# One row tile in ninety fetched row by row by SyncE instead of by a GpSimd gather

## The chip, the cores and the metric

The kernel runs on one core of a Trainium2 chip. The core has five engines that run side by side, each with its own instruction queue, executed in order: TensorE (PE, matrix products and transposes), VectorE (DVE), ScalarE (ACT), GpSimd (POOL) and SyncE (SP, which here only issues transfers). Sixteen DMA engines move the data between the large memory (HBM) and the on-chip memory (SBUF)[...]. Engines signal one another by semaphores. The metric is the device time of one execution in microseconds (us), the median of several runs.

## The reference

A recommender model scores 16,384 samples. Each sample has 69 fields, and each field names a row of an embedding table of 100,001 rows of 96 floats (384 bytes). A label names one more row, the query.

```python
u = emb[batch_user]                      # 16384 x 69 x 96
q = broadcast(emb[batch_label])
z = concatenate([q, u, q - u, q * u])
h = dice(z @ W1 + b1, a1)                # 384 -> 64
att = (h @ W2 + b2) @ W3 + b3            # one weight per row
pre = where(batch_user < ITEM_NUM, u * att, 0)
pooled = einsum('gf,bfe->bge', window, pre)       # 10 groups of fields
x = concatenate([pooled, ql])            # 11 * 96
# two more dense layers with dice (200, 80), then one output
```

So more than 1.1 million rows of the table are read at random places, and everything else is done on them.

## The kernel before

**Tiling.** The samples are cut into 32 blocks of 512 (`NBLK`, `BLK`). A block has 69 chunks (`NCH`): a chunk is 512 embedding rows, four row tiles of 128 rows, one row per SBUF partition. In the 64 main chunks of a block a chunk holds 64 fields of 8 samples; the other five chunks of a block hold one of the last fields for all 512 samples. Altogether there are 2208 chunks or 8832 row tiles. A step of the plan handles two chunks, so there are 1104 steps (`NPAIR`), 34.5 to a block.

**One step.** `fetch` (L301) allocates a row buffer `u` of eight row tiles and, for each of them, issues a gather on GpSimd (L312, through the helper `gather` at L256 to L262, so that its instructions stand under L257) and a TensorE transpose (L313) of the 128 x 96 tile into PSUM. A gather is an indirect DMA: GpSimd reads 128 indices from a column of the index tile `ids`, and the rows land on 128 partitions. After four transposes VectorE multiplies the chunk by the query (`quT`, L316) and ScalarE copies it (`uT`, L325). Two steps later `hidden` (L328) makes the hidden layer from both, ScalarE and VectorE finish it (L344 to L346); three and more steps later the attention weights are made (`attend_rows`, `spread`), and seven steps later (`POOL_LAG`) `pool` (L387) multiplies the row tiles, read a second time from `u`, by the weights (L397). The pool of row buffers has 14 of them (`upool`, L130). When a block is complete its dense layers (`top1` and after, L427 on) are spread over the next ten steps.

**Order of work.** The order is written out by hand: `at(step, ...)` (L530) puts pieces of work into a plan, and the plan is emitted step by step (L594). Each engine gets its instructions in that order; what an engine does next depends on its own queue and on the semaphores alone. The kernel's transfers are issued by two engines: GpSimd issues all gathers (8832 of row tiles, and 128 of label rows in `head_gather`, L271, four per block, 14 steps ahead of the block), SyncE issues the index loads, the weights at the start and the two stores at the end. `load_ids` (L144) loads the indices of four blocks at once into one of two buffers, 20 steps ahead of the first of these blocks (L565).

Of the kernel before, what the change touches and what calls it, by code (L numbers as in the profile page):

```python
# [1 line left out]

# [7 lines left out]

F32 = mybir.dt.float32
I32 = mybir.dt.int32
AF = mybir.ActivationFunctionType
ALU = mybir.AluOpType
PSUM = bass.MemoryType.PSUM

P = 128
B, F, E, G = 16384, 69, 96, 10  # L40
ITEM_NUM = 100000
# [5 lines left out]
NBLK = B // BLK  # L47
FM = 64
NTAIL = F - FM
NS = BLK // FM  # L50
NMAIN = BLK // NS
NCH = NMAIN + NTAIL
# [12 lines left out]
EARLY = 20  # L65

CLOSE = 8


class Pack:  # L70


    def __init__(self, **shapes):
        self.places, self.width = {}, 0
        for name, (row, n, m) in shapes.items():
            self.places[name] = slice(row, row + n), slice(self.width, self.width + m)
            self.width += m
# [37 lines left out]
def rec_kernel(  # L115
# [3 lines left out]
    idx: bass.AP,  # L119
    emb: bass.AP,  # L120
    rows: bass.AP,
    near: bass.AP,
    far: bass.AP,
    out: bass.AP,
):
    nc = tc.nc

    const = ctx.enter_context(tc.tile_pool(name="const", bufs=1))
    ipool = ctx.enter_context(tc.tile_pool(name="ipool", bufs=2))
# [10 lines left out]

    ids = {0: const.tile([P, NCOL], I32, name="ids0")}
    nc.sync.dma_start(out=ids[0], in_=idx0)

    def load_ids(n):  # L144

        t = ipool.tile([P, NIDS, NCOL], I32, tag="ids", name=f"ids{n}")
        nc.sync.dma_start(out=t.rearrange("p b n -> p (b n)"), in_=idx[(n - 1) // NIDS])
        for k in range(NIDS):
            ids[n + k] = t[:, k, :]


    wn = const.tile([P, NEAR.width], F32, name="wn")
    nc.sync.dma_start(out=wn, in_=near)
# [3 lines left out]
    ident = const.tile([P, P], F32, name="ident")  # L157
# [26 lines left out]
    for i in range(2):  # L184
        t = const.tile([E + 1, BLK], F32, name=f"qT{i}")
# [70 lines left out]
    def gather(table, dst, index):  # L256
        nc.gpsimd.indirect_dma_start(  # L257
            out=dst,
            out_offset=None,
            in_=table,  # L260
            in_offset=bass.IndirectOffsetOnAxis(ap=index, axis=0),
        )  # L262

    def chunk(c):

        n, k = divmod(c, NCH)
        if n == NBLK - 1 and k >= EARLY:
            k = NMAIN + k - EARLY if k < EARLY + NTAIL else k - NTAIL
        return n, k

    def head_gather(n):  # L271

# [28 lines left out]
    def fetch(i, between=None):  # L301

        u = upool.tile([P, 8, E], F32, tag="u", name=f"u{i}")
        uT = []
        quT = tpool.tile([E, 2, 512], F32, tag="quT", name=f"quT{i}")
        for j in range(2):
            if j == 1 and between:
                between()
            n, k = chunk(2 * i + j)
            ptr = ps_tr.tile([E, 512], F32, tag="tr", name=f"ptr{i}_{j}")  # L310
            for t in range(4):
                gather(rows, u[:, 4 * j + t, :], ids[n][:, 4 * k + t : 4 * k + t + 1])  # L312
                nc.tensor.transpose(ptr[:, t * P : (t + 1) * P], u[:, 4 * j + t, :], ident)  # L313
            q = qTs[n % 2][0:E]
            if k < NMAIN:
                nc.vector.tensor_tensor(  # L316
                    quT[:, j, :].rearrange("e (s f) -> e s f", f=FM),
                    ptr.rearrange("e (s f) -> e s f", f=FM),
                    by_field(q[:, k * NS : (k + 1) * NS]),
                    ALU.mult,  # L320
                )
            else:
                nc.vector.tensor_tensor(quT[:, j, :], ptr, q[:, 0:BLK], ALU.mult)
            uT.append(room(k))
            nc.scalar.copy(uT[j][0:E], ptr)  # L325
        return u, uT, quT

    def hidden(i, uT, quT):  # L328

        ph = ps_h.tile([P, 512], F32, tag="h", name=f"ph{i}")  # L330
        places = [chunk(2 * i + j) for j in range(2)]
        sums = [ph[j * H1 : (j + 1) * H1, :] for j in range(2)]
        for (n, k), p in zip(places, sums):
            if k >= NMAIN:
                nc.tensor.matmul(p, Cq, qTs[n % 2], start=True, stop=False)  # L335
        for j, ((n, k), p) in enumerate(zip(places, sums)):
            if k < NMAIN:
                nc.tensor.matmul(p, As[n % 2][:, k // 4, :], uT[j], start=True, stop=False)  # L338
            else:
                nc.tensor.matmul(p, A, uT[j][0:E], start=False, stop=False)  # L340
        for j, p in enumerate(sums):
            nc.tensor.matmul(p, Wp, quT[:, j, :], start=False, stop=True)  # L342
        y = ypool.tile([P, 512], F32, tag="y", name=f"y{i}")
        nc.scalar.activation(y, ph, AF.Sigmoid, scale=S_DICE)  # L344
        nc.scalar.activation(y, y, AF.Identity, bias=a1c, scale=na1c)  # L345
        nc.vector.tensor_mul(y, ph, y)  # L346
        return y
# [9 lines left out]

    def attend_tail(i, j, y, uT):

        n, k = chunk(2 * i + j)  # L360
        pa = ps_x.tile([E, 512], F32, tag="x", name=f"pa{i}_{j}")
        nc.tensor.matmul(pa, vrep[j * H1 : (j + 1) * H1, :], y[j * H1 : (j + 1) * H1, :], start=True, stop=True)  # L362
        nc.vector.scalar_tensor_tensor(pres[n][:, k - NMAIN, :], pa, bb[0:E], uT[j][0:E], ALU.add, ALU.mult)  # L363
# [23 lines left out]
    def pool(i):  # L387

        u, rw = us.pop(i), rws.pop(i)
        todo = [(j, *chunk(2 * i + j)) for j in range(2)]  # L390
        todo = [(j, n, k) for j, n, k in todo if k < NMAIN]
        if not todo:
            return
        pa = ps_acc.tile([E, 2, NS, G], F32, tag="acc", name=f"acc{i}")
        for j, n, k in todo:
            for t in range(4):
                nc.tensor.matmul(  # L397
                    pa[:, j, 2 * t : 2 * t + 2, :].rearrange("e n g -> e (n g)"),
                    u[:, 4 * j + t, :],
                    rw[:, t, j, :],  # L400
                    start=True,
                    stop=True,
                )
        if len(todo) == 2:
            _, n, k = todo[0]
            nc.vector.tensor_copy(  # L406
                pooled[n][:, :, k * NS : (k + 2) * NS].rearrange("e g s -> e s g"),
                pa.rearrange("e j s g -> e (j s) g"),
            )
        else:  # L410
            j, n, k = todo[0]
            nc.vector.tensor_copy(
                pooled[n][:, :, k * NS : (k + 1) * NS].rearrange("e g s -> e s g"), pa[:, j]
            )

    def dice(x, g, p, b, weights):

        sb, sa, sna = weights
        nc.scalar.activation(g, p, AF.Sigmoid, bias=sb, scale=S_BN * S_DICE)
        nc.scalar.activation(g, g, AF.Identity, bias=sa, scale=sna)  # L420
        nc.vector.scalar_tensor_tensor(x, p, b, g, ALU.add, ALU.mult)  # L421
# [78 lines left out]
    def pool_of(k):  # L500
        return lambda: pool(k)
# [4 lines left out]
    def tails_of(k):  # L506
        def work():
            uT = hs.pop(k)[0]
            for j in range(2):
                if chunk(2 * k + j)[1] >= NMAIN:  # L510
                    attend_tail(k, j, ys[k], uT)

        return work

    def fetch_of(k, between=()):
        def work():
            for j in range(2):
                n = chunk(2 * k + j)[0]
                if n not in pooled:
                    pooled[n] = bpool.tile([E, G, BLK], F32, tag="pooled", name=f"pooled{n}")  # L520
                    pres[n] = xpool.tile([E, NTAIL, BLK], F32, tag="pre", name=f"pre{n}")
            u, uT, quT = fetch(k, lambda: [w() for w in between])
            us[k], hs[k] = u, (uT, quT)

        return work
# [3 lines left out]

    def at(step, *work):  # L530
        plan.setdefault(step, []).extend(work)

    c = NPAIR - CLOSE
    for i in range(c):
# [6 lines left out]
        if i >= 2:  # L541
            at(i, hidden_of(i - 2))
        if i < c - CLOSE:
            if i >= POOL_LAG:
# [16 lines left out]
    for n in range(NBLK):  # L561
        first, end = n * NCH // 2, ((n + 1) * NCH - 1) // 2
        if n > 0:
            if n % NIDS == 1:
                at(first - 20, lambda n=n: load_ids(n))  # L565
            at(first - 14, lambda n=n: qs.__setitem__(n, head_gather(n)))
            at(first - 11, lambda n=n: head_turn(n, qs.pop(n)))
            at(first - 9, lambda n=n: head_rows(n))
        if n < NBLK - 2:
            for s, work in enumerate(top_steps(n, slice(0, BLK))):  # L570
                at(end + POOL_LAG + 4 + s, work)
        elif n == NBLK - 2:
            for s, work in enumerate(top_steps(n, slice(0, BLK))):
                at(end + POOL_LAG + s // 2, work)
# [9 lines left out]
    d = NPAIR  # L584
# [75 lines left out]
```

## Time and profile before

| what | value |
|---|---|
| median of 3 runs | 11251.05 us (11247.6 to 11253.1) |
| span of the profiled execution, first to last instruction | 11239.3 us |
| lies around the span (median less span) | 11.75 us |
| TensorE busy, share of the span | 9082.8 us, 81% |
| GpSimd busy | 8465.4 us, 75% |
| VectorE, ScalarE busy | 3014.3 us, 3188.3 us |
| row gathers on GpSimd | 8832, 945 ns each |
| from issue of a gather to its landing, median | 2.5 us |
| share of the 16 DMA engines taken by the gathers | 18.7% |
| granted clock of TensorE, mean | 0.727 |

The time of the profiled execution is known as its span; no other time of that execution is given, and the runs of the median are executions of their own.

A row of a group of instructions reads: line, engine, operation, what it writes and reads, how many; busy time in us and mean duration in ns; then the engine's idle time just ahead of them, and what ended most of that idle time. "issue" there means that nothing the profile shows was waited for. A row of the list of waits reads: who waited, for whom, total us, how often, the longest in us. A row of the timeline begins with start and duration in us, and the brackets hold the idle time ahead. "SPq" is SyncE's issuing of transfers, which isn't counted as busy.

### The profile page before, as it was taken

The numbers are of one execution on the slowest core, as the hardware profiler recorded it, in microseconds if no ns is written. First come the engines' busy times: TensorE is split into PE (matmuls) and PEld (weight loads), VectorE is DVE, ScalarE is ACT, GpSimd is POOL, SyncE is SP. The second block draws the span as 40 slices with busy tenths as digits, with TensorE's granted clock in tenths as the row PEclk, the third lists the DMA queues.
The fourth block names the chain that finished last, engine by engine and source line by source line (L and its number), as shares of the span: only waits on it lengthen the run. The fifth ranks groups of instructions, "written<-read, shape, count | busy, mean of one in ns | idle before, by whom it ended". The sixth has DMA issues, their size and how long they took to land.

```text
span 11239.3 us, 108444 instructions
## 1 busy us (share of the span) xinstructions
PE 9082.8 (81%) x41797; PEld 4395.1 (39%) x41797; DVE 3014.3 (27%) x5325; ACT 3188.3 (28%) x4969; POOL 8465.4 (75%) x8966
## 2 busy tenths in 40 slices
PE   7888888888878787877888778777787887888888
PEld 3333433333433333333333333333343333433335
DVE  3222222222222222222222222222222222222222
ACT  2222222222222222222222222222222222222223
POOL 7777777777777777777777777777777777777776
PEclk6767777677776777777777777777777767777767
DMA  2111111111111111111111111111111111111111
GB/s 49 40 40 40 40 40 42 40 40 40 40 42 40 40 40 40 42 40 40 40 40 42 40 40 40 40 42 40 40 40 40 42 40 40 40 40 40 40 40 35
DMA packets 288946, 454.19 MB, mean 40 GB/s; under 512 B 143538, under 2 KB 143922, under 8 KB 288306
## 3 DMA queue, kind: packets, MB, share of 16 engines
q0 software_dynamic: 286720, 440.98, 18.7%
q8 instruction: 335, 5.49, 0.2%
q1 hardware_dynamic: 1714, 6.28, 0.2%
q14 instruction: 177, 1.45, 0.0%
HBM read 446.61 MB, written 0.07 MB: 40 GB/s over the span
## 4 chain that ended last, share of the span: by engine, by line
POOL 51%; issue 23%; PE 15%; DMA 11%; ACT 0%; DVE 0%; POOLq 0%
POOL u L257 50%; DMA u<-in_rows,ids 11%; PE p L438 4%; PE acc L397 3%; PE ph L342 2%; PE ph L338 2%; PE ptr L313 2%; POOL q L257 1%; PE prow L353 1%; PE ph L335 1%; PE ph L340 0%; PE pc L290 0%; PE pa L362 0%; PE patt L370 0%; PE p L449 0%
## 5 line engine op out<-in xcount | busy, mean ns | idle before, releaser
L257 POOL DMA_INDIRECT u<-in_rows,ids x8832 | 8343.6, 945 | 2690.9 <-issue 2510.2
L313 PE MATMUL ptr<-ident,u 128*96 128x128 f32 x8832 | 2092.4, 336 | 2080.2 <-DMA u<-in_rows,ids 2066.4
L325 ACT COPY uT<-ptr 96x512 f32<-96x512 f32 x2208 | 1285.2, 582 | 4422.4 <-DVE quT L316 4069.1
L313 PEld LDWEIGHTS ptr<-ident,u 128*96 128x96 f32 x8832 | 1184.6, 150 | 2904.1 <-DMA u<-in_rows,ids 2460.6
L397 PEld LDWEIGHTS acc<-rw,u 128*96 128x96 f32 x16384 | 1746.1, 190 | 1206.4 <-issue 1059.7
L346 DVE TENSOR_TENSOR y<-ph,y 128x512 f32<-128x512 f32 x1104 | 763.5, 692 | 4885.1 <-ACT y L345 4703.4
L316 DVE TENSOR_TENSOR quT<-ptr,qT 96x512 f32<-96x512 f32 x2048 | 1375.9, 677 | 2183.2 <-PE ptr L313 2180.0
L397 PE MATMUL acc<-rw,u 128*96 128x20 f32 x16384 | 1852.9, 260 | 23.1 <-DVE rw L375 18.0
L338 PE MATMUL ph<-uT,A 128*64 128x512 f32 x4096 | 1688.2, 902 | 1.0 <-ACT uT L325 1.0
L342 PE MATMUL ph<-quT,wn 96*64 96x512 f32 x4416 | 1628.4, 809 | 0.0
L344 ACT ACTIVATE y<-ph 128x512 f32<-128x512 f32 x1104 | 659.4, 597 | 2971.7 <-PE ph L342 2962.3
L345 ACT ACTIVATE y<-y,wn,na1c 128x512 f32<-128x512 f32 x1104 | 898.1, 814 | 37.3
L342 PEld LDWEIGHTS ph<-quT,wn 96*64 96x64 f32 x4416 | 447.5, 191 | 1070.4 <-issue 1069.8
L438 PE MATMUL p<-pooled,wf 96*100 96x512 f32 (+1 forms) x1400 | 706.2, 654 | 0.0
L338 PEld LDWEIGHTS ph<-uT,A 128*64 128x64 f32 x4096 | 269.0, 179 | 616.0 <-issue 609.8
L406 DVE COPY pooled<-acc 96x160 f32<-96x160 f32 x1008 | 419.9, 417 | 129.4 <-PE acc L397 129.4
L353 PE MATMUL prow<-y,v 128*32 128x512 f32 x2208 | 452.4, 894 | 0.3 <-DVE y L346 0.3
L438 PE MATMUL p<-pre,V 96*100 96x512 f32 (+1 forms) x700 | 398.9, 717 | 2.7 <-DVE x L421 2.3
L438 PEld LDWEIGHTS p<-pooled,wf 96*100 96x100 f32 x1400 | 265.6, 202 | 341.2 <-issue 341.2
L375 DVE SCALAR_TENSOR_TENSOR rw<-patt,bb,wn 128x320 f32<-128x320 f32 x554 | 277.8, 543 | 221.2 <-PE patt L370 220.3
L355 ACT COPY row<-prow 128x512 f32<-128x512 f32 (+1 forms) x277 | 161.8, 584 | 314.5 <-PE prow L353 314.2
L370 PE MATMUL patt<-ident,row 128*128 128x128 f32 x1108 | 231.2, 347 | 15.9 <-DVE pre L363 15.2
(66 smaller groups left out, 2227.6 us busy)
## 6 DMA issues: line engine op xcount, KB each, us to landing
u<-in_rows,ids POOLq DMA_INDIRECT x8832, 2.5
ids<-in_idx SPq DMA_DIRECT2D x8, 560.0 KB, 3.7
q<-in_emb,ids POOLq DMA_INDIRECT x128, 2.5
wf<-in_far SPq DMA_DIRECT2D x1, 1209.0 KB, 7.8
wn<-in_near SPq DMA_DIRECT2D x1, 236.0 KB, 2.7
ids<-in_idx SPq DMA_DIRECT2D x1, 140.0 KB, 2.2
out<-r SPq DMA_DIRECT2D x1, 63.5 KB
out<-r SPq DMA_DIRECT2D x1, 0.5 KB
```

The lines of the kernel that those rows point to most:

```text
L257: nc.gpsimd.indirect_dma_start(out=dst, out_offset=None, in_=table, in_offset=bass.IndirectOffsetOnAxis(ap=index, axis=0),)
L313: nc.tensor.transpose(ptr[:, t * P : (t + 1) * P], u[:, 4 * j + t, :], ident)
L316: nc.vector.tensor_tensor(quT[:, j, :].rearrange("e (s f) -> e s f", f=FM), ptr.rearrange("e (s f) -> e s f", f=FM), by_field(q[:, k * NS ...
L325: nc.scalar.copy(uT[j][0:E], ptr)
L338: nc.tensor.matmul(p, As[n % 2][:, k // 4, :], uT[j], start=True, stop=False)
L342: nc.tensor.matmul(p, Wp, quT[:, j, :], start=False, stop=True)
L344: nc.scalar.activation(y, ph, AF.Sigmoid, scale=S_DICE)
L345: nc.scalar.activation(y, y, AF.Identity, bias=a1c, scale=na1c)
L346: nc.vector.tensor_mul(y, ph, y)
L353: nc.tensor.matmul(pr[32 * k : 32 * (k + 1), :], v2, ys[b + k], start=True, stop=True)
L397: nc.tensor.matmul(pa[:, j, 2 * t : 2 * t + 2, :].rearrange("e n g -> e (n g)"), u[:, 4 * j + t, :], rw[:, t, j, :], start=True, stop=True,)
L438: nc.tensor.matmul(p1, w[:, h * DH : (h + 1) * DH], x, start=(k == 0), stop=(k == KTOP - 1))
```

## The change

98 of the 8832 row tiles are no longer gathered by GpSimd. They are the fourth tile (`SLOT` = 3) of the second chunk of steps 9, 20, 31, ... 1076. For each of them SyncE issues 128 transfers of one row each, 384 bytes, from the table to one partition of a ring of four buffers (`ring`, 4 x 384 bytes on each partition). The row's byte offset is taken from a register. The offsets are prepared once: the row numbers of the 98 tiles come in as an extra input (one tile per partition, 128 numbers), VectorE multiplies them by three and shifts them left by seven, which makes 384 times the number. SyncE loads 32 of them at a time into registers.

Each row transfer adds 16 to one of eight semaphores, which the tiles use in turn. TensorE has one wait per such tile, ahead of the tile's transpose, for the count that all 128 rows make together; transpose and pooling product then read the ring buffer in place of a part of `u`. The fetch of a tile stands in SyncE's queue at the place of the step six ahead of its use, and SyncE itself waits until the readers of the ring buffer four tiles earlier are done. The index loads, which share SyncE's queue, move from 20 to 50 steps ahead of their first block. Settings for a second fetcher on ScalarE are in the code with an empty list.

The diff, cut to its core (in `hidden`, `attend_tail` and other places `chunk` is only renamed `chunk_of`):

```diff
+ROW_BYTES = 4 * E
+SLOT = 3
+SP_CHUNKS = [2 * (11 * s + 9) + 1 for s in range(98)]
+SP_RING = 4
+NSEM = 8
...
+    row_bytes = rows.bitcast(U8).rearrange("(o n) k -> o (n k)", o=1)
...
+    offsets = const.tile([P, NSB, P], I32, name="offsets")
+    nc.sync.dma_start(out=offsets.rearrange("p b r -> p (b r)"), in_=single_rows)
+    nc.vector.tensor_scalar(offsets, offsets, 3, None, ALU.mult)
+    nc.vector.tensor_scalar(offsets, offsets, 7, None, ALU.logical_shift_left)
...
+        def load(self, s, start):
+            i, stop = self.first + s, min(P, start + self.group)
+            _, values = nc.values_load_multi_w_load_instructions(
+                offsets[i % P : i % P + 1, i // P, start:stop],
+                engines=[self.kind],
...
+        def fetch(self, s, start, stop):
+            b, k = self.buffers[s % len(self.buffers)], s % NSEM
+            for r in range(start, stop):
+                if r % self.group == 0:
+                    self.load(s, r)
+                d = self.engine.dma_start(
+                    out=ring[r : r + 1, b], in_=row_bytes[:, bass.ds(self.values[r], ROW_BYTES)]
+                ).then_inc(self.sems[k], 16)
...
+            if stop == P:
...
+                self.given[k] += 16 * P
+                places[self.chunks[s]] = b, self.sems[k], self.given[k]
...
+    def wait_for_single(c, t):
+        if single(c, t):
+            nc.tensor.wait_ge(*single(c, t)[1:])
+
+    def read_rows(op, out, u, c, t, other, **how):
+        at = single(c, t)
+        ins = op(out, ring[:, at[0]].bitcast(F32) if at else u[:, 4 * (c % 2) + t, :], other, **how)
...
             for t in range(4):
-                gather(rows, u[:, 4 * j + t, :], ids[n][:, 4 * k + t : 4 * k + t + 1])
-                nc.tensor.transpose(ptr[:, t * P : (t + 1) * P], u[:, 4 * j + t, :], ident)
+                if single(2 * i + j, t):
+                    wait_for_single(2 * i + j, t)
+                else:
+                    gather(rows, u[:, 4 * j + t, :], ids[n][:, 4 * k + t : 4 * k + t + 1])
+                read_rows(nc.tensor.transpose, ptr[:, t * P : (t + 1) * P], u, 2 * i + j, t, ident)
...
+    by_sync = Singles("sp", nc.sync, mybir.EngineType.SP, SP_CHUNKS, 0, range(SP_RING), 32)
+    for s, m in enumerate(SP_CHUNKS):
+        at(max(0, m // 2 - 6), lambda s=s: by_sync.fetch(s, 0, P))
...
-                at(first - 20, lambda n=n: load_ids(n))
+                at(max(0, first - 50), lambda n=n: load_ids(n))
...
+    ring = nc.alloc_sbuf_tensor("ring", [P, SP_RING + ACT_RING, ROW_BYTES], U8).ap()
```

More of the change, by code (lines that the diff above doesn't have):

```diff
@@ L34 @@
 I32 = mybir.dt.int32
+U8 = mybir.dt.uint8
 AF = mybir.ActivationFunctionType
@@ L67, with chunk_of @@
 CLOSE = 8
+ROW_BYTES = 4 * E
+SLOT = 3
+SP_CHUNKS = [2 * (11 * s + 9) + 1 for s in range(98)]
+SP_RING = 4
+ACT_CHUNKS = []
+ACT_RING = 0
+ACT_ROWS = 12
+ACT_STEPS = -(-P // ACT_ROWS)
+SINGLES = SP_CHUNKS + ACT_CHUNKS
+NSB = (len(SINGLES) + P - 1) // P
+NSEM = 8
+def chunk_of(c):
+    n, k = divmod(c, NCH)
+    if n == NBLK - 1 and k >= EARLY:
+        k = NMAIN + k - EARLY if k < EARLY + NTAIL else k - NTAIL
+    return n, k
 class Pack:
@@ L121, in rec_kernel @@
     rows: bass.AP,
+    single_rows: bass.AP,
     near: bass.AP,
@@ L124, in rec_kernel @@
     out: bass.AP,
+    ring: bass.AP,
 ):
     nc = tc.nc
+    row_bytes = rows.bitcast(U8).rearrange("(o n) k -> o (n k)", o=1)
     const = ctx.enter_context(tc.tile_pool(name="const", bufs=1))
@@ L262, in gather, with __init__ @@
         )
[L264 to L269, printed above, removed]
+    places = {}
+    class Singles:
+        def __init__(self, name, engine, kind, chunks, first, buffers, group):
+            self.name, self.engine, self.kind, self.group = name, engine, kind, group
+            self.chunks, self.first, self.buffers = chunks, first, buffers
+            self.sems = [tc.alloc_semaphore(f"{name}{k}") for k in range(NSEM)]
+            self.given = [0] * NSEM
+        def load(self, s, start):
[3 more added lines that the diff above has]
+                engines=[self.kind],
+                min_val=0,
+                max_val=ITEM_NUM * ROW_BYTES,
+                skip_runtime_bounds_check_because="offsets of rows of the table",
+            )
+            self.values = dict(enumerate(values, start))
+        def fetch(self, s, start, stop):
[6 more added lines that the diff above has]
+                ).then_inc(self.sems[k], 16)
+                tc.no_tile_sem_insts.add(d.ins.name)
+                tc.declare_no_dep(d.ins, group=f"ring{b}", reason="a buffer's readers have waited for its rows")
+                fresh.setdefault(b, []).append(d.ins)
+            if stop == P:
+                for ins in fresh.pop(b):
+                    tc.add_to_no_dep_group(f"ring{b}", ins)
+                self.given[k] += 16 * P
+                places[self.chunks[s]] = b, self.sems[k], self.given[k]
@@ L271, in head_gather, with single @@
+    fresh = {}
+    def single(c, t):
+        return places.get(c) if t == SLOT else None
+    def wait_for_single(c, t):
[4 more added lines that the diff above has]
+        ins = op(out, ring[:, at[0]].bitcast(F32) if at else u[:, 4 * (c % 2) + t, :], other, **how)
+        if at:
+            tc.declare_no_dep(ins.ins, group=f"ring{at[0]}", reason="waited for by semaphore")
     def head_gather(n):
@@ L308, in fetch @@
                 between()
-            n, k = chunk(2 * i + j)
+            n, k = chunk_of(2 * i + j)
             ptr = ps_tr.tile([E, 512], F32, tag="tr", name=f"ptr{i}_{j}")
             for t in range(4):
-                gather(rows, u[:, 4 * j + t, :], ids[n][:, 4 * k + t : 4 * k + t + 1])
-                nc.tensor.transpose(ptr[:, t * P : (t + 1) * P], u[:, 4 * j + t, :], ident)
+                if single(2 * i + j, t):
[3 more added lines that the diff above has]
+                read_rows(nc.tensor.transpose, ptr[:, t * P : (t + 1) * P], u, 2 * i + j, t, ident)
             q = qTs[n % 2][0:E]
@@ L330, in hidden @@
         ph = ps_h.tile([P, 512], F32, tag="h", name=f"ph{i}")
-        places = [chunk(2 * i + j) for j in range(2)]
+        places = [chunk_of(2 * i + j) for j in range(2)]
         sums = [ph[j * H1 : (j + 1) * H1, :] for j in range(2)]
@@ L358, in attend_tail @@
     def attend_tail(i, j, y, uT):
-        n, k = chunk(2 * i + j)
+        n, k = chunk_of(2 * i + j)
         pa = ps_x.tile([E, 512], F32, tag="x", name=f"pa{i}_{j}")
@@ L389, in pool @@
         u, rw = us.pop(i), rws.pop(i)
-        todo = [(j, *chunk(2 * i + j)) for j in range(2)]
+        todo = [(j, *chunk_of(2 * i + j)) for j in range(2)]
         todo = [(j, n, k) for j, n, k in todo if k < NMAIN]
@@ L396, in pool @@
             for t in range(4):
-                nc.tensor.matmul(
+                read_rows(
+                    nc.tensor.matmul,
                     pa[:, j, 2 * t : 2 * t + 2, :].rearrange("e n g -> e (n g)"),
-                    u[:, 4 * j + t, :],
+                    u,
+                    2 * i + j,
+                    t,
                     rw[:, t, j, :],
@@ L509, in work @@
             for j in range(2):
-                if chunk(2 * k + j)[1] >= NMAIN:
+                if chunk_of(2 * k + j)[1] >= NMAIN:
                     attend_tail(k, j, ys[k], uT)
@@ L517, in work @@
             for j in range(2):
-                n = chunk(2 * k + j)[0]
+                n = chunk_of(2 * k + j)[0]
                 if n not in pooled:
@@ L620, in side_by_side @@
         return a.reshape(n, -1, a.shape[1]).transpose(1, 0, 2).reshape(-1, n * a.shape[1])
+    singles = np.zeros((P, NSB, P), np.int32)
+    for s, m in enumerate(SINGLES):
+        n, k = chunk_of(m)
+        singles[s % P, s // P] = ids[n][:, 4 * k + SLOT]
     arrays = {
@@ L626 @@
         "rows": np.concatenate([x["emb"][:ITEM_NUM], np.zeros((1, E), np.float32)], axis=0),
+        "single_rows": singles.reshape(P, -1),
         "near": NEAR.fill(
@@ L655 @@
     out = nc.dram_tensor("out_0", (B, 1), F32, kind="ExternalOutput").ap()
+    ring = nc.alloc_sbuf_tensor("ring", [P, SP_RING + ACT_RING, ROW_BYTES], U8).ap()
     with tile.TileContext(nc) as tc:
-        rec_kernel(tc, *args, out)
+        rec_kernel(tc, *args, out, ring)
     r = run_bass_kernel_spmd(nc, [arrays], core_ids=[0])
```

## The prediction, made before the change was run

> **What bounds the kernel now.** I read the page's busy times first, then GpSimd's waits, its timeline, the stretches around an index load, and last SyncE's rows. The page:
>
> ```profile
> PE 9082.8 (81%) x41797; PEld 4395.1 (39%) x41797; DVE 3014.3 (27%) x5325; ACT 3188.3 (28%) x4969; POOL 8465.4 (75%) x8966
> ```
>
> TensorE looks busiest, and GpSimd (POOL) seems to have a quarter of its time free. The costliest groups correct that:
>
> ```profile
> L257 POOL DMA_INDIRECT u<-in_rows,ids x8832 | 8343.6, 945 | 2690.9 <-issue 2510.2
> L313 PE MATMUL ptr<-ident,u 128*96 128x128 f32 x8832 | 2092.4, 336 | 2080.2 <-DMA u<-in_rows,ids 2066.4
> ```
>
> GpSimd's idle time is "issue": it waits for nothing visible. TensorE's idle time is waiting for gathered rows. GpSimd's list of waits says whether a buffer ever holds it up:
>
> ```profile
> POOL u L257 <- issue: 2510.2, 8239, 0.3
> POOL u L257 <- DMA u<-in_rows,ids: 120.7, 396, 0.3
> POOL u L257 <- PE ptr L313: 43.6, 143, 0.3
> ```
>
> The longest idle is 0.3 us under every name, so no release is late; 0.3 us is the gap between two gathers. The timeline, while SyncE's first 560 KB index load is issued (at 1753.4):
>
> ```profile
> 1753.39 0.94 POOL L257 DMA_INDIRECT u<-in_rows,ids  x1 [0.30 <-issue]
> 1754.64 0.94 POOL L257 DMA_INDIRECT u<-in_rows,ids  x1 [0.30 <-issue]
> 1755.89 0.94 POOL L257 DMA_INDIRECT u<-in_rows,ids  x1 [0.30 <-issue]
> ```
>
> One gather starts every 1.25 us. Over the run: second label gather at 4.62, last gather at 11196.52, 8958 intervals, hence 1.249 us each. So 8960 gathers (8832 row tiles, 128 label tiles) make 11,191 us of the 11,239.3; about 5 us lie ahead and 42.8 us behind (last TensorE work and store). GpSimd's issue rate bounds the kernel. The chain of waits gives TensorE 15% only because it hops to a semaphore's sender; GpSimd's gap there is still 0.3.
>
> [...]
>
> **The change, part by part.**
>
> *Removed.* 98 gathers at GpSimd: 98 x 1.249 = 122.4 us, all on the bounding path, since its gap never stretches for anything else. Nothing else leaves.
>
> *SyncE's row DMAs*, 98 x 128 = 12,544, ahead of TensorE by a ring of four. Time available per tile: eleven steps have 88 row gathers, 11 x 128/1104 = 1.3 label gathers and one less for the change: 88.3 x 1.249 = 110.2 us, or 861 ns per row. Cost per row: SyncE's issues of index loads (shortest, median, longest in ns) and its last store (start and duration in us) are
>
> ```profile
> L147 SPq DMA_DIRECT2D ids<-in_idx x8: 327/328/432, 2.1 to 8756.5; - x8
> ```
>
> ```profile
> 11237.14 0.25 SPq L474 DMA_DIRECT2D out<-r  x1
> ```
>
> A 128-partition load takes 328 ns, a 512 B single row 250. Consecutive starts at 0.75, 1.21 and 1.68 with durations 0.41 and 0.42 leave 50 ns between. The address comes from a register, 32 loaded at a time, four times per tile. The trace has neither register load nor register-addressed DMA. [...] SyncE is then idle a third of the time, held by the ring, and the cost is nothing because 88 gathers cover it. Without that cover each microsecond over 110 counts 98 times.
>
> *First tile.* Needed at step 9, last gather at about 8.4 + 79 x 1.249 + 2.5 = 110 us. SyncE starts after the offsets and their two VectorE operations, about 8 us, plus 74 = 82. Covered; at the limit of 861 ns it would come at 118, 8 us late once.
>
> *Ring.* A buffer's last reader is the pooling seven steps after its transpose: tile s may begin at step 11(s-4)+16 and is wanted at 11s+9, 37 steps or 370 us for 74 us of work.
>
> *TensorE's counted wait*, 98 times. Behind it in TensorE's queue stand the transpose, the hidden-layer matmuls, later pooling, and so VectorE's product and ScalarE's copy. A passed wait is about 51 ns (the event-semaphore instructions on TensorE's queue): 98 x 0.051 = 5 us inside 2066 us of idle. Nothing. If rows were late, transposes would queue, then release row buffers late (14, pooled 7 steps later), and only then GpSimd.
>
> *Moved.* Eight index loads go from 20 to 50 steps ahead of their block, each behind one tile's rows at most in SyncE's queue. Each load must land by the label gather 14 steps ahead: 36 steps, 360 us, against 74 + 3.7 of landing. The buffer it overwrites is free 138 steps ahead of the block, so its wait doesn't block SyncE. *Offsets*: one more SyncE issue (0.46 us) ahead of the weights, two VectorE operations near the 0.2 us of their neighbours; GpSimd starts on the first index load, which stays ahead. Zero; bounds 0 to 1 us.
>
> *Traffic.* 17,920 packets per engine take 18.7% of 11,239.3 us, 117 ns each. [...] Bounds: -1 ns and +14 ns per gather (14 x 8862 = 124 us, the whole gain); a gain has no cause in view, so zero at the low end. The index load is the nearest row:
>
> ```profile
> 1753.00:1763.00 10.00, 7.57 (x9) 0.66 0.26 59
> 2000.00:3000.00 1000.00, 755.97 (x801) 0.72 0.19 40
> ```
>
> Columns: stretch, us, GpSimd busy and gathers, clock, DMA share, GB/s. Busy per us is 0.757 against 0.756 with half as much traffic again. I take 0.
>
> *Sum.* Span 11,239.3 - 122.4 = 11,116.9. The runs' median stands 11.75 us above the span; 11,251.05 - 122.4 = 11,128.7, or -1.09%.
>
> **Rivals.**
>
> *A, SyncE becomes the bound (slower).* One mechanism: the register load is paid per row, or a register-addressed DMA is dearer than any here, beyond 861 ns per row. [...] For it: neither operation has a row. Against: all shown SyncE issues are 250 to 430 ns, and 32 values come by one call. From 861 ns on SyncE sets the end; at 871 (122.4 us over 12,544 rows more) the gain is gone.
>
> *B, contention eats it.* [...] For it: in the first 130 us gathers stretch to 1.04-1.09 us beside two-input VectorE work, so that span isn't fixed. Against: [...] the load above did nothing.
>
> *C, TensorE takes over.* 9082.8 us busy plus waits; if its long runs (18.7 us without a gap from 5018.5, where the top layers run) filled the buffers, perhaps half the gain stays: 11,190. Against: GpSimd isn't held once; taking 122 from 2066 us of idle changes little.
>
> *D, the change doesn't do what it says*: rows still gathered as well. The branch in fetch excludes it.
>
> **How the numbers follow.** Forecast 0.80 (own range 11,121 to 11,145: run-to-run spread of 6 us, and gathers up to 2 ns longer). A 0.10. B 0.07, of which 0.03 faster still, 0.03 within 0.2%, 0.01 slower. C 0.03, faster. About 0.2%, 22 us, is what a measurement here can tell from no change. Faster 0.80 + 0.03 + 0.03 = 0.86, same 0.03, slower 0.11. Range 11,118 to 11,190: it takes in C and B's half, and leaves out A and B's rest, about 0.14.
>
> **What would show it.** 8734 row gathers at 945 ns with 0.3 idle, none longer; GpSimd's last start near 11,074; SyncE's row issues at 0.4 to 0.7 us and SyncE waiting for a pooling matmul; nearly no TensorE wait on the counted semaphore. Wrong if row issues come over 861 ns back to back (A), if a gather's mean or gap rises by some ns (B), or if GpSimd's longest idle exceeds 0.3 (C).

## The result and the profile after

The changed kernel takes 11,127.48 us (median of four runs, 11,126.79 to 11,132.49) against 11,252.08 (11,247.6 to 11,253.46): a ratio of 0.9892, 95% interval 0.9878 to 0.9906, or 124.6 us less. The forecast was 11,129. The span of the profiled execution is 11,130.7 us, 108.6 less than before; its own time is 11,132.49, so only 1.8 us lie around a span. In a later run of the kernel before it is the same 1.8 us (13,431.36 against 13,429.6). Of the 11.75 us found between its span and its median, some 10 were thus a profiled execution faster than the median.

The page of the changed kernel, its busy times and the same two groups as before:

```profile
PE 8988.0 (81%) x41797; PEld 4347.6 (39%) x41797; DVE 3007.8 (27%) x5327; ACT 3188.7 (29%) x4969; POOL 8384.2 (75%) x8868
...
L266 POOL DMA_INDIRECT u<-in_rows,ids x8734 | 8262.2, 946 | 2664.2 <-issue 2478.2
L325 PE MATMUL ptr<-ident,u 128*96 128x128 f32 x8734 | 2054.2, 333 | 2068.9 <-DMA u<-in_rows,ids 2054.0
```

98 gathers are gone, those left cost the same, and TensorE still waits for gathered rows as much as before. GpSimd's list of waits:

```profile
POOL u L266 <- issue: 2478.2, 8124, 0.3
POOL u L266 <- DMA u<-in_rows,ids: 124.5, 408, 0.3
POOL u L266 <- PE ptr L325: 43.0, 141, 0.3
```

No row gather waits for a buffer: 0.3 us is again their longest idle, under every name. (The prediction's "under every name" leaves out one wait of 1.9 us, there as here: that of the first label gather for the first index load.) What took the work over, the instructions that touch the ring (shortest, median and longest in ns, then first and last start in us):

```profile
L301 SPq MOVE ring<-in_rows x12544: 29/29/29, 5.8 to 10435.2; - x200
L301 SPq DMA_DIRECT2D ring<-in_rows x12544: 227/228/423, 5.9 to 10435.3; - x200
...
L325 PE MATMUL ptr<-ident,ring x98: 272/421/421, 110.2 to 10821.5; 128*96 128x128 f32 x98
```

and the register loads, four to a tile:

```profile
L286 SPq TENSOR_LOAD <-offsets x392: 2031/2175/2378, 3.7 to 10423.0; - x196
```

A row is a 29 ns move and a 228 ns transfer; row starts lie 322 ns apart (median, worked out from the starts in the trace). SyncE's timeline (start, duration):

```profile
5035.85 48.96 SPq L301 DMA_DIRECT2D ring<-in_rows  x128
5085.17 0.37 SPq L151 DMA_DIRECT2D ids<-in_idx  x1
5148.47 91.50 SPq L301 DMA_DIRECT2D ring<-in_rows  x231
```

A tile takes 49 us of SyncE, the first register load apart (2.2), out of 110. For the rest it is held by the ring, which its list of waits shows:

```profile
SPq L301 <- PE ptr L325: 5326.8, 87, 119.9
```

The list names the transpose that comes next in TensorE's queue; in the trace a tile's first row starts 0.3 us after the pooling product of the tile four before it (288.29 after 288.0, 400.28 after 400.0), which is the ring buffer's last reader.

TensorE's list of waits has no row for the ring: each counted wait was already met. The DMA queues:

```profile
q0 software_dynamic: 283584, 436.15, 18.7%
q1 hardware_dynamic: 26946, 11.21, 0.4%
```

The rows' queue, 0.2% of the sixteen engines' time before, has 0.4% now.

### The profile page after: what moved, and what is told of

Same layout as the page of the kernel before. It is cut to its first block, busy times and chain, and to the rows that moved or that the text cites. A ratio compares the mean times of both kernels' runs of the same rounds, so it can differ in the third digit from the quotient of the medians.

```text
span 11130.7 us, 133926 instructions
## 1 busy us (share of the span) xinstructions
PE 8988.0 (81%) x41797; PEld 4347.6 (39%) x41797; DVE 3007.8 (27%) x5327; ACT 3188.7 (29%) x4969; POOL 8384.2 (75%) x8868
## 3 DMA queue, kind: packets, MB, share of 16 engines
q0 software_dynamic: 283584, 436.15, 18.7%
q1 hardware_dynamic: 26946, 11.21, 0.4%
## 4 chain that ended last, share of the span: by engine, by line
POOL 51%; issue 23%; PE 15%; DMA 11%; ACT 0%; DVE 0%; POOLq 0%
POOL u L266 50%; DMA u<-in_rows,ids 11%; PE p L502 4%; PE acc L325 3%; PE ph L403 2%; PE ph L399 2%; PE ptr L325 2%; POOL q L266 1%; PE prow L414 1%; PE ph L396 0%; PE pa L423 0%; PE pc L348 0%; PE ph L401 0%; PE patt L431 0%; PE p L513 0%
## 5 line engine op out<-in xcount | busy, mean ns | idle before, releaser
L325 PE MATMUL ptr<-ident,u 128*96 128x128 f32 x8734 | 2054.2, 333 | 2068.9 <-DMA u<-in_rows,ids 2054.0
L325 PEld LDWEIGHTS ptr<-ident,u 128*96 128x96 f32 x8734 | 1161.4, 149 | 2869.7 <-DMA u<-in_rows,ids 2423.0
L325 PEld LDWEIGHTS acc<-rw,u 128*96 128x96 f32 x16202 | 1706.4, 188 | 1192.1 <-issue 1034.7
L325 PE MATMUL acc<-rw,u 128*96 128x20 f32 x16202 | 1812.9, 259 | 23.8 <-DVE rw L436 18.6
```

The costliest lines, as they stand in the source:

```text
L325: ins = op(out, ring[:, at[0]].bitcast(F32) if at else u[:, 4 * (c % 2) + t, :], other, **how)
```

## Experiments

Each of the four sets brought its own runs of the kernel before. They ran on chips 7, 8, 14 and 11; on which chip the pair above (the first pair) ran isn't on record. On all four the kernel before took 13,344 to 13,447 us (medians), 19% more. So only ratios within a set are compared, and what was different in these runs comes first. Whether that belongs to the chips or to something else in these sets isn't known, and no experiment ran under the conditions of the first pair.

### The kernel before, there

> The kernel before itself, for its profile beside the other runs of this set: no part changed. Own theory (only GpSimd's issue counts): about 11,252 us, gathers spaced 1.249 us. If the row transfers make gathers dearer (the profile of the changed kernel has them at 1.251 us), the spacing here stays at 1.249 and that of the kernels without row transfers too; if the 1.251 comes from the execution or the chip, it moves without them.

Measured 13,431 us, one run. Its GpSimd waits:

```profile
POOL u L257 <- issue: 2409.2, 7893, 0.6
POOL u L257 <- PE ptr L313: 1002.5, 213, 40.1
POOL u L257 <- remote: 980.3, 312, 6.0
```

The gathers cost what they did (943 ns), and where nothing intervenes their starts lie 1.248 us apart; but 664 of the 8959 intervals are longer than 1.3 us and hold 2145 us beyond the normal spacing, which is the difference between the spans (13,429.6 - 11,239.3 = 2190) but for 2%. GpSimd is held up, up to 40 us at a time. A good half of it (1370 us, summed over the list) has TensorE's instructions named, most of them transposes; most of the rest has "remote", a releaser that the profile doesn't identify. TensorE's timeline (start, duration, idle ahead):

```profile
5056.94 0.59 PE L340 MATMUL ph<-uT,A 96*64 96x512 f32 x1 [0.40 <-issue]
5058.35 0.59 PE L340 MATMUL ph<-uT,A 96*64 96x512 f32 x1 [0.82 <-issue]
...
5060.48 1.01 PE L342 MATMUL ph<-quT,wn 96*64 96x512 f32 x1 [1.48 <-issue]
5061.90 1.01 PE L342 MATMUL ph<-quT,wn 96*64 96x512 f32 x1 [0.40 <-issue]
5064.00 1.01 PE L342 MATMUL ph<-quT,wn 96*64 96x512 f32 x1 [1.09 <-issue]
```

For some ten microseconds at a time its instructions start only 1.4 or 2.1 us apart, in steps of about 0.7, waiting for nothing visible; then it runs normally. Starts of TensorE's instructions (matmuls, weight loads, semaphore waits) that lie 0.66 to 0.74 us apart occur 187 and 177 times in the two traces of the first pair, and 1077 to 2283 times in each of the twelve traces of the sets. What does this is not known. In these sets, then, TensorE sets part of the pace, and the cover on which the forecast rested, its idle time, is partly used up. They show what the change costs without that cover.

The expectation also asked whether the 1.251 us spacing of the changed kernel's profile came from the row traffic. It didn't: with gaps over 1.3 us left out, the spacing was 1.2481 here and 1.2481 and 1.2507 in the two runs without any row transfer (below), and 1.2483 and 1.2509 in the two with row transfers and all gathers. The page's row of gathers in the second run of each kind, first rows left out, then gathers kept:

```profile
L266 POOL DMA_INDIRECT u<-in_rows,ids x8734 | 8262.0, 946 | 4679.2 <-issue 2189.5
```

```profile
L266 POOL DMA_INDIRECT u<-in_rows,ids x8832 | 8332.5, 943 | 4909.0 <-issue 2172.4
```

The one without row traffic has the dearer gathers. The two values belong to the execution.

### Gathers removed, nothing in their place

```diff
+    nc.vector.memset(ring.bitcast(F32), 0.0)
...
     def wait_for_single(c, t):
-        if single(c, t):
-            nc.tensor.wait_ge(*single(c, t)[1:])
+        return
...
     for s, m in enumerate(SP_CHUNKS):
-        at(max(0, m // 2 - 6), lambda s=s: by_sync.fetch(s, 0, P))
+        places[m] = s % SP_RING, None, None
```

> 98 gathers removed and nothing fetched in their place: no row transfer, no register load, no counted wait; TensorE reads a ring of zeros, so 98 row tiles are left out of the result. Own theory (SyncE's work is wholly hidden): the same as the changed kernel, 11,127 us within 5. Rival (the row transfers cost something by contention): faster than 11,127; the 14 us by which the profiled span missed the forecast would put it near 11,113.

> As in the first set, on another chip, since the kernel before ran 19% slower there, with pauses on every engine: 98 gathers removed, nothing fetched in their place, TensorE reads a ring of zeros (98 row tiles are left out of the result). Own theory (SyncE's work is wholly hidden): the changed kernel's ratio to before, 0.9892, or about 11,128 us, within 5 us. Rival (row transfers cost by contention): faster by up to 14 us.

Measured 0.9895 (0.9869 to 0.9921) and 0.9884 (0.9861 to 0.9907). 98 of 8960 gathers are 1.094%, a ratio of 0.9891. So the removal is worth its share of the gathers even here. It is also the ratio of the changed kernel in the first pair: there nothing measurable was paid for the rows. On a slower chip the changed kernel itself stands at 1.0047 (below), so there the own theory, "the same as the changed kernel", falls.

### Gathers kept, rows fetched as well

```diff
                 if single(2 * i + j, t):
                     wait_for_single(2 * i + j, t)
-                else:
-                    gather(rows, u[:, 4 * j + t, :], ids[n][:, 4 * k + t : 4 * k + t + 1])
+                gather(rows, u[:, 4 * j + t, :], ids[n][:, 4 * k + t : 4 * k + t + 1])
```

> All 8832 gathers stay, and SyncE fetches its 98 tiles as well, with TensorE's waits and reading from the ring. Own theory (all gain is the removed gathers): the time before, 11,252 us within 5. Rival (contention): slower, by up to 14 us. If the gain came from something else than the removed gathers, it would be below 11,240.

> As in the first set, where it came out 1.4% over the kernel before on the disturbed chip: all 8832 gathers stay and SyncE fetches its 98 tiles as well. Own theory (the whole gain is the removed gathers, row transfers cost nothing where GpSimd alone is the bound): ratio 1.000, about 11,252 us within 10. Rival (row transfers or the 98 counted waits cost by themselves): 1.014 again, about 11,405 us.

Measured 1.0136 (1.0112 to 1.016) and 1.0155 (1.0132 to 1.0178). On these chips the rows are not free: 183 and 194 us. My theory, as far as it was meant for any run, falls; the rival's direction is right, its first size (14 us) far too small.

### The changed kernel, there

> The changed kernel itself, beside the kernel before on whatever chip this set gets: no part changed. Own theory where GpSimd alone is the bound: 0.9892 of before. Where the engines pause as on the chips of the first two sets, removal gave 0.9889 and the rows by themselves 1.0145; if these add, the changed kernel stands at 1.003 of before there, and its gain depends on TensorE having slack; if the gain holds there too (below 0.995), the two don't add.

Measured 1.0047 (1.0032 to 1.0062): 0.5% slower. The product of the two halves is 0.989 x 1.0145 = 1.0033, within the interval near its lower end; the measurement agrees with parts that add. SyncE pauses as TensorE does; the rows' instructions:

```profile
L301 SPq MOVE ring<-in_rows x12544: 1/29/1403, 5.9 to 12680.1; - x200
L301 SPq DMA_DIRECT2D ring<-in_rows x12544: 2/228/1399, 6.0 to 12680.2; - x200
```

A move that was 29 ns without exception now takes up to 1403. From a tile's first row to its last it is 90 us on average (from the starts in the trace), not 49. That still fits eleven steps, which at this kernel's mean gather spacing of 1.504 us are 88.3 x 1.504 = 133 us. TensorE's list of waits has no row for the ring, and no transpose starts sooner than 22.8 us after the issue of its tile's last row. So it isn't SyncE's lateness that costs here.

The pauses of the two engines share a beat. Of the 649 pauses of SyncE (starts 0.66 to 0.74 us apart) that have a like pause of TensorE within 0.35 us of them, half a step, 635 have it within 0.1 us. So both seem to wait for something that they have in common; the trace doesn't name it.

### What of the rows costs

Two kernels keep all gathers, the ring, the 98 counted waits and TensorE's reading from the ring. In the first each tile comes by one transfer of 128 neighbouring rows of the table; the rows asked for are left out. The second adds 25,088 SyncE instructions that do nothing, as many as the moves and transfers of the rows (two of the 512 waits of a tile share an instruction: 133,727 instructions in the trace against 108,639).

```diff
-            for r in range(start, stop):
-                if r % self.group == 0:
-                    self.load(s, r)
-                d = self.engine.dma_start(
-                    out=ring[r : r + 1, b], in_=row_bytes[:, bass.ds(self.values[r], ROW_BYTES)]
-                ).then_inc(self.sems[k], 16)
+            d = self.engine.dma_start(
+                out=ring[:, b], in_=rows.bitcast(U8)[s * P : (s + 1) * P]
+            ).then_inc(self.sems[k], 16)
...
-                self.given[k] += 16 * P
+                self.given[k] += 16
```

and in the second kernel, beside that,

```diff
+            for r in range(4 * P):
+                self.engine.wait_ge(self.sems[k], self.given[k])
```

> All gathers kept, as in the gathers-kept runs, but each of SyncE's 98 tiles comes by one transfer of 128 neighbouring rows of the table (the rows asked for are left out): the same ring, the same bytes, the same 98 counted waits and reads from the ring, yet 98 SyncE instructions instead of 25,088 and no register loads. Where the gathers-kept kernel stood at 1.0145 of before: if the single-row issuing costs it (SyncE's instructions or the 12,544 small packets), 1.000 here; if the counted waits and the ring's reading on TensorE cost it, 1.0145 again. Where GpSimd alone is the bound, own theory: 1.000.

> The same with 25,088 more SyncE instructions that do nothing: waits that have long been passed (the rows asked for are left out as before). If SyncE's instruction stream by itself costs, about 1.0145 again; if the small packets or register loads cost, 1.000 as with the single transfers. Own guess: the instruction stream, 1.01 or more, since the pauses hit every queue that issues many short instructions.

Measured 0.9997 (0.9984 to 1.001) and 1.0095 (1.0067 to 1.0122). The counted waits, the ring's readers and the bytes cost nothing measurable, even where TensorE has little slack. Nor do the small packets that carry the rows: the first kernel's trace has the same 12,544 packets of 384 bytes as the rows had, and only the packets of 4 bytes are fewer, 16 to a tile instead of 128. About two thirds of the rows' cost come back with idle SyncE instructions alone, if the chips are alike: 131 us between the medians, 125 us between the two profiled spans, and 124 us more in what GpSimd's intervals over 1.3 us hold beyond the normal spacing (2265 against 2141). GpSimd's list of waits, first without, then with the idle instructions:

```profile
POOL u L266 <- remote: 991.4, 314, 5.9
POOL u L266 <- PE ptr L322: 936.2, 200, 39.8
```

```profile
POOL u L266 <- remote: 1085.3, 429, 6.0
POOL u L266 <- PE ptr L324: 952.8, 211, 44.3
```

So a stream of short instructions on one engine lengthens what holds GpSimd up, on these chips. Only in part is TensorE named for it: summed over the list, waits with its instructions named grow by 67 us, those with an unidentified releaser by 94. The idle instructions bring one more thing with them. The DMA queue that the profile calls "instruction" moves 1.6 MB more, 64 bytes for each of the 25,088; again without and with them:

```profile
q14 instruction: 178, 1.46, 0.0%
```

```profile
q14 instruction: 374, 3.06, 0.1%
```

Whether running them or these bytes is what costs isn't separated. Nor is the last third, which may lie in the 4-byte packets, register loads, the rows' scattered places in the table, or in moves and transfers that are dearer than waits: the interval's upper end, 1.0122, reaches into that of the first gathers-kept run. How one queue's instructions slow another's stays open.

### A ring of one

```diff
-SP_RING = 4
+SP_RING = 1
...
-        at(max(0, m // 2 - 6), lambda s=s: by_sync.fetch(s, 0, P))
+        at(max(0, m // 2 - 3), lambda s=s: by_sync.fetch(s, 0, P))
```

> One ring buffer instead of four, the fetch of a tile standing three steps ahead of its use in the program instead of six: SyncE can begin a tile only once the pooling of the one before is done, 4 steps or 40 us ahead of its use, for 49 us of row transfers and 2 of landing. TensorE then waits some 11 us at each of 98 tiles, 1080 us in all. Own theory (TensorE has 2054 us of idle time and 14 row buffers between it and GpSimd): the same as the changed kernel, 11,127 us within 15, GpSimd's longest idle still 0.3. Rival (a wait in TensorE's queue lies on the path): up to 12,200 us.

> As in the first set, where it came out 14% over the kernel before: one ring buffer, so TensorE waits some 11 us or more at each of 98 tiles. Own theory (2054 us of TensorE idle time and the row buffers cover it where GpSimd alone is the bound): the changed kernel's time, 11,128 us within 15. Rival (TensorE's wait and the fetch it holds back feed each other: a late TensorE pools late, so SyncE starts late): each tile costs its uncovered wait and more, 98 x 11 = 1080 us or beyond, over 12,200 us.

Measured 1.14 (1.1365 to 1.1435) and 1.1407 (1.1379 to 1.1435). In the second, TensorE's and GpSimd's lists of waits:

```profile
PE ptr L325 <- DMA ring<-in_rows: 2719.5, 90, 56.7
```

```profile
POOL u L266 <- PE ptr L325: 2980.7, 296, 43.5
```

TensorE waits 30 us at 90 tiles, not 11: a tile takes 77 us from its first row to its last here, with a register load of 2 us ahead and 1.3 us (median) behind until its transpose, against four steps of 32 gathers at 1.488 us, 48 us. Against the changed kernel, from another set, it is (1.1407 - 1.0047) x 13,347 = 1815 us, 18.5 us per tile: two thirds of the wait reach the end. The rival was right where TensorE is short of slack, and its 1080 us were too few; whether the 2054 us of idle time of the first pair would swallow 11 us per tile was not tried.

### One tile per six steps

```diff
-SP_CHUNKS = [2 * (11 * s + 9) + 1 for s in range(98)]
+SP_CHUNKS = [2 * (6 * s + 9) + 1 for s in range(179)]
...
-NSEM = 8
+NSEM = 16
```

> 179 tiles by SyncE, one per six steps instead of 98, one per eleven; 16 semaphores instead of 8. The profile has a tile's 128 rows at 49 us on SyncE; six steps give (48 + 0.8 - 1) x 1.249 = 59.7 us. Own theory (SyncE has room, each gather removed is 1.249 us): 11,252 - 179 x 1.249 = 11,028 us, within 10. Rival (contention or waits grow with the rows): 11,050 or above.

> As before: 179 tiles, one per six steps. On the chip of the second set a tile's 128 rows took 78 us of SyncE instead of 49, more than the 59.7 us of six steps, and the time came out 10% over before: 179 x 78 us and the ends. Own theory: where a tile takes 49 us it is hidden, 11,252 - 179 x 1.249 = 11,028 us (ratio 0.980); where it takes about 78, ratio 1.10 again. Rival (row traffic itself costs, whatever SyncE's pace): over 1.0 in either case.

Measured 1.0994 (1.0964 to 1.1024) and 1.099 (1.0962 to 1.1019). The second run's rows, and TensorE's wait with the largest total:

```profile
L301 SPq DMA_DIRECT2D ring<-in_rows x22912: 1/228/1405, 6.3 to 14293.0; - x200
```

```profile
PE ptr L325 <- DMA ring<-in_rows: 2570.1, 151, 45.4
```

From the first row to the last it is 14,287 us, 79.8 per tile, with no more between two tiles than the 2.5 us of a register load: SyncE has become the bound. This is rival A of the prediction with another cause, a SyncE that pauses instead of a dear register load. Six steps are 47.8 x 1.488 = 71 us at the pace of the kernel before here. Under the conditions of the first pair, where a tile takes 49 us of 59.7, this kernel should gain 179 x 1.249 = 224 us; it got no run there, and that is not shown.

## Why the prediction was right, and where

**Removed.** Right: 98 x 1.249 = 122.4 us forecast, 124.6 between the medians. In the profile the last gather starts at 11,088.8 instead of 11,074, since its gathers lie 1.251 us apart, 0.13% more; 8862 of them make the 15 us. The experiments put that down to the execution; the two profiled executions also lie on opposite sides of their medians, that of the kernel before some 10 us under, that of the changed kernel 5 us over.

**SyncE's row.** Right side, wrong size. The 74 us per tile, 0.58 us per row, were the author's estimate: the price of a register load in it was not shown by the trace of the kernel before. Measured are 0.322 + 2.175/32 = 0.39. The transfer was priced as a 128-partition load (328 ns) where the single-row store (250) was the nearer row and 228 was measured; a register load measured 68 ns per register (2175 ns for 32). One term was too small: 50 ns between transfers, where 322 - 228 = 94 were measured, a move of 29 ns among them that the sum didn't have.

**First tile, ring, counted wait, moved loads.** Right: the first transpose from the ring starts at 110.2 us (forecast 110), SyncE waits 5327 us for the ring's readers, TensorE never for the rows that SyncE fetches, and no wait for index loads appears on GpSimd beyond the first one.

**Traffic.** Right in the sum, at zero. What packets a row makes was not shown by the trace of the kernel before. In that of the changed kernel each row transfer carries one element of 384 bytes. The queue has 26,946 packets; the kernel with the rows left out has 1858; the difference, 25,088, is two per row, one of 384 bytes and one of 4. The queue's share grew by 0.2%, and that of the gathers' queue stayed at 18.7%.

**Rivals.** B, gathers made dearer by the row traffic, fell: their spacing doesn't follow it (1.2481 and 1.2507 us without rows, 1.2483 and 1.2509 with them). C fell in the first pair: the longest idle of a row gather stayed 0.3. A fell there, with twice the room it needed, and came true in another kernel in the slower sets. D fell: 8734 row gathers are left. In the slower sets GpSimd is held up with TensorE named, as C has it, in the kernel before already.

**What it lacked.** It took GpSimd's place as the only bound for a property of the kernel. It is one of the kernel in runs where TensorE keeps its pace, as in those whose profile it was read from; where TensorE and SyncE pause, the same change is 0.5% slower. The step that fails there is "the cost is nothing because 88 gathers cover it": it asked only whether SyncE is in time, and had no term for what 25,088 further SyncE instructions do to the other engines. With the cover gone they and their transfers cost 1.4 to 1.6%.

## What to carry to other kernels

An engine that works from the start to the end with a gap that nothing else ever stretches (0.3 us here) is the bound, whatever its busy share says (here 75%). A removed instruction is then worth its spacing, not its duration: 98 x 1.249 us, and not 98 x 0.945. Before moving work to an idle queue, price both its room per period and what its instruction count does where the other engines have no slack; in the first pair both were free, in the slower sets the second took back the gain (1.0047). A period that just fits one pace leaves nothing for runs in which engines pause: at 49 us of work for 59.7 us of time the kernel came out 10% slower there, while at 49 of 110 the rows stayed in time.

## What was unexpected of the hardware

In all four sets of experiments the engines ran through phases in which TensorE's and, where it had rows to fetch, SyncE's instructions started in steps of about 0.7 us, on one beat where both paused at once, with 19% more time for the same kernel; 25,088 idle instructions on SyncE made another 0.95%. A register load from SBUF took 68 ns per register in groups of 32, and a register-addressed transfer of one row 228 ns, less than any transfer that SyncE issued in the kernel before (254 ns and up).
